# One sum of GpSimd put earlier, the PSUM pools swapped, and a convolution tap given to DVE, in a Hyena layer with experts

## The chip, the cores and the metric

The kernel runs on one core of a Trainium2 chip. Its engines are TensorE (PE, with its weight loads as PEld), VectorE (DVE), ScalarE (ACT), GpSimd (POOL) and SyncE (SP), which here issues most of the transfers. The metric is the device time of one execution in microseconds (us). A profile of one execution stands beside it.

## The reference, cut to what matters

The input is x, 8192 tokens of 512 channels. A first layer projects it to three streams of 512 channels, runs a short convolution of three taps over time on each, multiplies two of them to a gate, convolves the gate with a filter as long as the sequence, and multiplies the outcome by the third stream:

```python
u = x @ W_in + b_in                       # 8192 x 1536
up = pad(u, ((0, 0), (2, 2), (0, 0)))     # over time
uc = up[:, 0:length] * w[:, 0] + up[:, 1:length+1] * w[:, 1] + up[:, 2:length+2] * w[:, 2] + b
x0, x1, v = split(uc, 3)
v = v * x1                                # the gate
k = _gen_filter(...)                      # two sine layers, then the taps with a decay
v = _causal_fft_conv(v, k, filter_bias)
y = (v * x0) @ W_out + b_out
x = layernorm(x + y)
```

A second layer sends each group of 32 tokens to 32 experts in four sets and adds what they give, with a second layer norm. The change does not touch it.

## The kernel before, in words

The kernel has three stages, called one after the other from hyena_then_experts: project (the projection, the short convolution, the filter), convolve (the long convolution as Fourier products on PE) and experts.

**How project is tiled.** Tokens come in 8 blocks of 1024, and the 512 channels of each stream in two pairs (m) of two 128-channel tiles. A Quad is one block, one pair m and one stream s: two tiles of channels by two halves of 512 tokens. There are 8 x 2 x 3 = 48 of them, walked in the loop over j (from L464); r = j % 6 is the place within a block, r = 5 its last quad. A quad is computed in Strassen's way (Winograd's form): seven products in place of eight, each two matmuls of 128x128 by 128x512 (L327). They take sums of weight tiles (sums_of_win) and sums of token tiles:

```python
a, c = {"1": ("12", "11"), "2": ("22", "t1"), "3": ("22", "12"), "4": ("21", "t2")}[name]
x["t" + name] = t = wk.tile(..., bufs=2 if name == "1" else 1)
e.tensor_tensor(t, x[a], x[c], ALU.subtract)      # L206
```

So there are four sums for each block, t1 to t4, each a 128x1024 subtraction; t2, t3 and t4 have one buffer. The token tiles "11", "12", "21", "22" are loaded by SP (load_tokens, L194) into six buffers. The sums for block 0 are made on DVE at the start, those of later blocks on GpSimd: sum 1 in the turn r = 3 of the block before, sums 2, 3 and 4 in its turn r = 5, where also the tile "22" of the next block is loaded, after p1 of that turn.

**The order of a turn.** PE, DVE, ACT and GpSimd follow the order in which the program is written (manual_schedule); SP's order is made by the planner. A turn j issues: p1 (product of "11", copied out by ACT); what is left of the filter's work from the turn before (left); p2 and p6 (into one pair of PSUM banks; p2 reads "21", p6 reads t2; drained by DVE, L346); the short convolution of the quad before (before); p75 (t3, then t1; drained by DVE, L361 and L362); sums 2 and 3 where r = 5; a piece of the filter; p43 (t4 and "22"; drained by DVE, L369); sum 4 where r = 5.

**The short convolution of a quad** (short_convolution): ACT carries two columns over (L377, L378) and writes the tap of the newest token with the bias into four PSUM banks (L389). With on_dve false, ACT also writes the oldest tap into w in SBUF (L395, 128x1024), DVE adds the middle tap (L405) into a tile o in SBUF, and GpSimd adds o to w (L415 for the streams s = 1, 2; L419 for s = 0, where w is kept in two interleaved halves). With on_dve true, DVE adds the middle tap in place in PSUM (L405), and then the oldest tap with a second instruction that reads PSUM and writes w (L409). After that s = 0 is written to memory as x0 (L421), s = 1 is kept, and s = 2 is multiplied with it on GpSimd (L429) and written as the gate (L430). on_dve is true for s = 2 from j = 23 on. The last quad, j = 47, has s = 0; its short convolution stands behind the loop, with on_dve false.

**PSUM.** There are eight banks. In project a pool of four single banks (bank: p1, the filter, the short convolution) is opened first and one of two pairs of banks (pair: p26, p75, p43) second. When both are closed, convolve opens a pool of four pairs over all eight banks (banks, psum2, with reuse_waits="tile").

**The start of convolve.** over_n1 multiplies tiles of the filter's taps by a Fourier table (L552) into those pairs, 16 matmuls of 128x64 by 128x128 a pair (tile pa); DVE (L561) and ACT (L559) copy them in turn into place. That tile fills 192 KB of each partition, over the SBUF that project used.

Every matmul is in fp32 and has two records in the profile, so one product of a quad has four, and one pa tile 32.

Of the kernel before, what the change touches and what calls it, by code (L numbers as in the profile page):

```python
# [15 lines left out]
ALU = mybir.AluOpType  # L16
# [79 lines left out]
@with_exitstack  # L96
def hyena_then_experts(ctx: ExitStack, tc: tile.TileContext, i: dict, out: bass.AP):
    nc = tc.nc

    const = ctx.enter_context(tc.tile_pool(name="const", bufs=1))  # L100
    dram = ctx.enter_context(tc.tile_pool(name="dram", bufs=1, space=bass.MemoryType.DRAM))

    def load(pool, name):
        t = pool.tile(list(i[name].shape), F32, tag=name, name=name + "_sb")
        nc.sync.dma_start(out=t, in_=i[name])
        return t

    def in_dram(what, shape):
        return [dram.tile(shape, F32, tag=f"{what}{ct}", name=f"{what}{ct}") for ct in range(NCT)]


    y_dram = {
        (ct, n): dram.tile([P, BT], F32, tag=f"y{ct}_{n}", name=f"y{ct}_{n}")
        for ct in range(NCT)
        for n in range(NBLK)
    }


    with tc.tile_pool(name="pairs", bufs=2) as pairs, tc.tile_pool(name="in", bufs=3) as tables:
        kept = {  # L120
            name: const.tile(list(i[name].shape), F32, tag=name, name=name + "_sb")
            for name in ("chan", "c_in", "c_back")
        }
        between = in_dram("x0", [P, L]), in_dram("gate", [P, P, N2]), in_dram("taps", [P, P, N2])
        with (
            tc.tile_pool(name="psum1", bufs=4, space=bass.MemoryType.PSUM) as psum,
            tc.tile_pool(name="psum0", bufs=2, space=bass.MemoryType.PSUM) as psum0,
        ):

            def bank(name):  # L130
                return psum.tile([P, 512], F32, tag="ps", name=name)

            def pair(name):
                return psum0.tile([P, 2, TB], F32, tag="pair", name=name)

            project(tc, i, bank, pair, load, between, kept, pairs)
        with tc.tile_pool(
            name="psum2", bufs=4, space=bass.MemoryType.PSUM, reuse_waits="tile"
        ) as psum:

            def banks(name):
                return psum.tile([P, 1024], F32, tag="ps", name=name)

            convolve(tc, i, banks, kept, pairs, tables, between, y_dram)
    experts(tc, i, load, y_dram, out)


def project(tc, i, bank, pair, load, between, kept, small):
# [11 lines left out]
    with (  # L160
# [40 lines left out]
        def sum_of_tokens(b, x, name, e):  # L201
            a, c = {"1": ("12", "11"), "2": ("22", "t1"), "3": ("22", "12"), "4": ("21", "t2")}[name]
            x["t" + name] = t = wk.tile(
                [P, 2, TB], F32, tag=f"xs{name}", name=f"xs{name}_{b}", bufs=2 if name == "1" else 1
            )
            e.tensor_tensor(t, x[a], x[c], ALU.subtract)  # L206
# [166 lines left out]
        def short_convolution(q, on_dve):  # L373

            b, m, s = q.b, q.m, q.s
            now = carry[:, s, :, m]
            nc.scalar.copy(q.u[:, :, 0:2], now)  # L377
            nc.scalar.copy(now, q.u[:, :, 2 * TB : 2 * TB + 2])  # L378
            for half in range(2):
                ct = m + NP * half  # L380
                u = q.u[:, 1 - half]
                at = s * NCT + ct
                w = wk.tile([P, 2 * TB], F32, tag="w", name=f"w_{half}{q.nm}", bufs=5)

                by_half = lambda v: v.rearrange("p (a h b) -> p h a b", h=2, b=N2 // 2)
                pss = [bank(f"o_{half}_{n}{q.nm}") for n in range(2)]
                for n in range(2):
                    t0 = n * TB
                    nc.scalar.activation(  # L389
                        pss[n], u[:, t0 + 2 : t0 + 2 + TB], AF.Identity,  # L390
                        bias=bias[:, at : at + 1], scale=ch[:, at, 4:5],
                    )
                if not on_dve:
                    of = u[:, 0 : 2 * TB]
                    nc.scalar.activation(  # L395
                        w if s else w.rearrange("p (h a b) -> p h a b", h=2, b=N2 // 2),
                        of if s else by_half(of), AF.Identity, scale=ch[:, at, 2:3],
                    )
                for n in range(2):
                    t0, ps = n * TB, pss[n]  # L400
                    if on_dve:
                        o = ps
                    else:
                        o = wk.tile([P, TB], F32, tag="o", name=f"o_{half}_{n}{q.nm}", bufs=4)
                    nc.vector.scalar_tensor_tensor(  # L405
                        o, u[:, t0 + 1 : t0 + 1 + TB], ch[:, at, 3:4], ps, ALU.mult, ALU.add
                    )
                    if on_dve:
                        nc.vector.scalar_tensor_tensor(  # L409
                            w[:, t0 : t0 + TB], u[:, t0 : t0 + TB], ch[:, at, 2:3], o,  # L410
                            ALU.mult, ALU.add,
                        )
                    elif s:
                        wn = w[:, t0 : t0 + TB]
                        nc.gpsimd.tensor_tensor(wn, o, wn, ALU.add)  # L415
                    else:
                        a = TB // N2
                        wn = w.rearrange("p (h a b) -> p h a b", h=2, b=N2 // 2)[:, :, n * a : (n + 1) * a]
                        nc.gpsimd.tensor_tensor(wn, by_half(o), wn, ALU.add)  # L419
                if s == 0:  # L420
                    nc.sync.dma_start(  # L421
                        out=x0_dram[ct].rearrange("c (h n) -> c h n", h=2)[:, :, b * TB : (b + 1) * TB],
                        in_=w.rearrange("c (h n) -> c h n", h=2),
                    )
                elif s == 1:
                    gates[half] = w
                else:
                    gate = gates.pop(half)
                    nc.gpsimd.tensor_tensor(gate, gate, w, ALU.mult)  # L429
                    nc.sync.dma_start(  # L430
                        out=gate_dram[ct][2 * b * TB // N2 : 2 * (b + 1) * TB // N2].rearrange(
                            "a c b -> c a b"
                        ),
                        in_=gate.rearrange("c (a b) -> c a b", b=N2),
                    )
# [28 lines left out]
        for j in range(n_quads):  # L464
            b, r = divmod(j, 3 * NP)
            m, s = r // 3, (1, 2, 0)[r % 3]
            if r == 0 and b:
                x, nxt = nxt, None
            if j < 3:
                q = quads[j]  # L470
            else:
                q = Quad(b, m, s, x)
                q.p1()
                if r == 5 and nxt:
                    load_tokens(b + 1, nxt, ("22",))
            for f in left:
                f()
            if j >= 2:
                q.p2()
                q.p6()  # L480
            if before:
                short_convolution(before, before.s == 2 and j > filter_until)
            if j == 1:
                sums_of_win(1, nc.gpsimd)
            q.p75()
            if r == 5 and nxt:
                sum_of_tokens(b + 1, nxt, "2", nc.gpsimd)
                sum_of_tokens(b + 1, nxt, "3", nc.gpsimd)
            if j < filter_until:
                n = n_filter * (j + 1) // filter_until - n_filter * j // filter_until  # L490
            else:
                n = taps_by_turn[r]
            parts, rides = [f(*args) for f, *args in rides[:n]], rides[n:]
            left = []
            if j >= filter_until and parts:
                parts.pop(0)()()
            q.p43()
            for on_dve in parts:
                left.append(on_dve())
            before = q  # L500
            if b + 1 < NTB // 2:
                if r == 1:
                    nxt = {}
                    load_tokens(b + 1, nxt, ("12", "11", "21"))
                if r == 3:
                    sum_of_tokens(b + 1, nxt, "1", nc.gpsimd)
                if r == 5:
                    sum_of_tokens(b + 1, nxt, "4", nc.gpsimd)
        for f in left:
            f()  # L510
        short_convolution(before, False)


CC = 16
# [661 lines left out]
```

## Time and profile before

| what | before |
|---|---|
| median of 3 runs | 2284.95 us (2281.37 to 2286.8) |
| the profiled execution, its own time | 2284.01 us |
| its span, first to last instruction | 2282.2 us |
| mean granted TensorE clock | 0.965 |
| busy, PE, DVE, ACT, POOL | 2084.2, 1366.3, 800.5, 683.7 us |
| project, from the start to the first matmul of convolve | to 702.05 us |
| convolve, to the first matmul of the experts | to 1417.46 us |

A row of a timeline gives the start in us, the length in us, the engine, the line of the kernel, the operation, the tiles it writes and reads, and how many instructions were merged. What stands in brackets is the idle time of the engine before the row and the instruction that ended it ("<-POOL xs L206": the engine stood until POOL had written xs at L206). A row of the costliest groups ends with busy time, mean ns of one instruction, and the group's idle time with its main releaser. The granted clock is the share of full TensorE clock that the chip let through.

### The profile page before, as it was taken

Reading aid. Unit: us, or ns where it says so; the run is one execution under the profiler, and the core shown is the slowest. Engines: PE = TensorE matmul, PEld = TensorE weight load, DVE = VectorE, ACT = ScalarE, POOL = GpSimd, SP = SyncE. Lnnn points to the kernel's source line nnn. Section 1 sums busy time; section 2 is a strip of 40 time slices with the busy share of each in tenths; the row PEclk is TensorE's granted clock in tenths of the full one; section 3 lists DMA queues with packets and bytes.
Section 4 is the critical chain, followed back from the end, with each engine's and each line's share of the span. In section 5 each row is a group of like instructions: output and inputs, shape, how many; then the busy total and the mean of one; then the engine's idle time right before and its main releaser. Section 6 shows DMA issues by size and latency. Waiting matters only on the chain. (4 is left out here: it accounts for less than half of the span.)

```text
span 2282.2 us, 65661 instructions
## 1 busy us (share of the span) xinstructions
PE 2084.2 (91%) x29472; PEld 1440.4 (63%) x29472; DVE 1366.3 (60%) x1860; ACT 800.5 (35%) x1278; POOL 683.7 (30%) x610
## 2 busy tenths in 40 slices
PE   8898999999998999999999998889988999898765
PEld 3343344444447989999999998355555556555643
DVE  6676776766664643553463463456566666666647
ACT  2444445555553321321331231121343234234333
POOL 3545646766751430340250160211100100110000
PEclk9999999999999999999999999999998999899887
DMA  5312312532434736645655574526663754665373
GB/s 150 102 47 65 94 55 74 193 130 74 139 129 130 223 132 220 211 162 196 194 205 178 177 244 164 157 77 196 217 201 127 246 188 140 196 231 189 114 264 127
DMA packets 188197, 362.61 MB, mean 159 GB/s; under 512 B 78422, under 2 KB 101852, under 8 KB 184844
## 3 DMA queue, kind: packets, MB, share of 16 engines
q1 hardware_dynamic: 182412, 340.05, 46.2%
q10 hardware_dynamic: 5504, 18.35, 2.1%
q8 instruction: 232, 3.80, 0.7%
q14 instruction: 49, 0.40, 0.1%
HBM read 274.47 MB, written 83.89 MB: 157 GB/s over the span
## 5 line engine op out<-in xcount | busy, mean ns | idle before, releaser
L327 PE MATMUL p<-xs,win 128*128 128x512 f32 x768 | 359.6, 613 | 18.6 <-POOL xs L206 16.3
L327 PEld LDWEIGHTS p<-xs,win 128*128 128x128 f32 x768 | 145.9, 194 | 205.2 <-issue 168.8
L327 PE MATMUL p<-xq,win 128*128 128x512 f32 x576 | 259.5, 598 | 7.6 <-DMA win<-in_W_in 5.1
L747 POOL TENSOR_TENSOR xt<-xt,b_outb_sb 128x512 f32<-128x512 f32 x64 | 82.6, 1291 | 608.0 <-DMA xt<-in_x 431.8
L749 PE MATMUL po<-wout,yt 128*128 128x512 f32 x512 | 242.5, 618 | 21.4 <-DVE x L753 18.1
L598 POOL TENSOR_TENSOR place<-t,hs 128x256 f32<-128x256 f32 x132 | 94.7, 718 | 471.9 <-DVE hs L596 470.1
L552 PE MATMUL pa<-c_in_sb,vk 128*64 128x128 f32 x4096 | 226.1, 274 | 9.1 <-DVE o L405 8.7
L552 PEld LDWEIGHTS pa<-c_in_sb,vk 128*64 128x64 f32 x4096 | 224.8, 138 | 10.5 <-DVE o L405 9.5
L576 PE MATMUL px<-place,tab 128*64 128x128 f32 x4096 | 227.8, 273 | 1.9 <-ACT place L559 1.9
L576 PEld LDWEIGHTS px<-place,tab 128*64 128x64 f32 x4096 | 226.2, 136 | 3.0 <-ACT place L559 2.9
L327 PEld LDWEIGHTS p<-xq,win 128*128 128x128 f32 x576 | 110.0, 192 | 149.8 <-issue 135.9
L749 PEld LDWEIGHTS po<-wout,yt 128*128 128x128 f32 x512 | 94.7, 195 | 133.4 <-issue 99.6
L415 POOL TENSOR_TENSOR w<-o,w 128x512 f32<-128x512 f32 x92 | 114.5, 1272 | 173.6 <-ACT w L395 126.4
L561 DVE COPY place<-pa 128x1024 f32<-128x1024 f32 x64 | 78.3, 1224 | 142.2 <-PE pa L552 136.1
L912 ACT COPY si<-pi 128x1024 f32<-128x1024 f32 x96 | 92.9, 1013 | 185.9 <-PE pi L903 128.8
L559 ACT COPY place<-pa 128x1024 f32<-128x1024 f32 x64 | 64.8, 1012 | 252.4 <-PE pa L552 246.6
L405 DVE SCALAR_TENSOR_TENSOR o<-u,chan_sb,o 128x512 f32<-128x512 f32 x192 | 135.8, 744 | 27.2 <-ACT o L389 27.2
L916 DVE STREAM_TRANSPOSE si<-si 128x2048 f32<-128x2048 f32 x48 | 108.1, 2290 | 69.7 <-ACT si L912 69.7
L389 ACT ACTIVATE o<-u,bias,chan_sb 128x512 f32<-128x512 f32 x192 | 141.0, 767 | 0.0
L609 PE MATMUL pz<-c_back_sb,place 64*128 64x128 f32 x2048 | 123.2, 283 | 14.4 <-POOL place L598 14.4
L609 PEld LDWEIGHTS pz<-c_back_sb,place 64*128 64x128 f32 x2048 | 122.5, 199 | 15.4 <-POOL place L598 15.4
L591 ACT COPY hs<-px 128x512 f32<-128x512 f32 x132 | 75.6, 573 | 156.6 <-PE px L576 151.2
(110 smaller groups left out, 3130.1 us busy)
## 6 DMA issues: line engine op xcount, KB each, us to landing
f<-in_f SPq DMA_DIRECT2D x160, 512.0 KB, 5.1
tab<-in_c_mid SPq DMA_DIRECT2D x64, 512.0 KB, 3.8
place<-in_c_out SPq DMA_DIRECT2D x64, 512.0 KB, 4.7
gate<-w SPq DMA_DIRECT2D x32, 512.0 KB, 4.1
x<-w SPq DMA_DIRECT2D x32, 512.0 KB, 3.0
taps<-taps SPq DMA_DIRECT2D x4, 4096.0 KB, 11.1
vk<-taps SPq DMA_DIRECT2D x32, 512.0 KB, 3.6
vk<-gate SPq DMA_DIRECT2D x32, 512.0 KB, 3.7
```

What stands on the lines that cost most here:

```text
L327: nc.tensor.matmul(ps, win[self.m][:, slot, self.s, k, :], self.x[tokens][:, k, :], start=(k == 0), stop=(k == 1),)
L389: nc.scalar.activation(pss[n], u[:, t0 + 2 : t0 + 2 + TB], AF.Identity, bias=bias[:, at : at + 1], scale=ch[:, at, 4:5],)
L405: nc.vector.scalar_tensor_tensor(o, u[:, t0 + 1 : t0 + 1 + TB], ch[:, at, 3:4], ps, ALU.mult, ALU.add)
L415: nc.gpsimd.tensor_tensor(wn, o, wn, ALU.add)
L552: nc.tensor.matmul(ps[r * 64 : (r + 1) * 64, c * N1 : (c + 1) * N1], vk[:, half * 8 + c, :], cin[:, r, :], start=True, stop=True,)
L576: nc.tensor.matmul(ps[h * 64 : (h + 1) * 64, j, :, r, :], tab[:, g % 2 * KC + j, r * 64 : (r + 1) * 64], both[:, :, g * KC + j, h * 64 : ( ...
L598: nc.gpsimd.tensor_tensor(o[:, 0], t[:, 0], hs[:, 1], ALU.subtract)
L609: nc.tensor.matmul(ps[:, h, c, :], spec[rows, r, c0 + c, :], cback[rows, r].rearrange("p q n -> p (q n)"), start=(r == 0), stop=(r == 1),)
L747: nc.gpsimd.tensor_tensor(xt, xt, bout, ALU.add)
L749: nc.tensor.matmul(ps, got["y"][:, ct, t % 2 * P : (t % 2 + 1) * P], wout[:, ct, :], start=(ct == 0), stop=(ct == NCT - 1),)
L912: nc.scalar.copy(o, pss[rr].rearrange("p (r q d) -> p r d q", r=2, q=4))
L916: nc.vector.transpose(turned[:, d].rearrange("p d g -> p (d g)"), stage[:, d].rearrange("p d e -> p (d e)"),)
```

## The change

It has three parts, in project and in hyena_then_experts.

1. In the turn r = 5 of a block, sum 2 of the next block is issued ahead of the short convolution of the quad before, right behind p2 and p6, and no longer behind p75. Sum 3 stays where it was.
2. The pool of pairs is opened ahead of the pool of single banks, so the pairs lie in the first four banks of PSUM and the single banks in the last four.
3. The last short convolution (j = 47, s = 0) is called with on_dve true, and gets a form of the second tap for s = 0 that writes the two interleaved halves of w with two instructions of 256 elements for each 512 tokens.

```diff
         with (
+            tc.tile_pool(name="psum0", bufs=2, space=bass.MemoryType.PSUM) as psum0,
             tc.tile_pool(name="psum1", bufs=4, space=bass.MemoryType.PSUM) as psum,
-            tc.tile_pool(name="psum0", bufs=2, space=bass.MemoryType.PSUM) as psum0,
         ):
...
-                    if on_dve:
+                    if on_dve and s == 0:
+                        a = TB // N2
+                        wv = w.rearrange("p (h a b) -> p h a b", h=2, b=N2 // 2)[:, :, n * a : (n + 1) * a]
+                        for h in range(2):
+                            nc.vector.scalar_tensor_tensor(
+                                wv[:, h], by_half(u[:, t0 : t0 + TB])[:, h], ch[:, at, 2:3],
+                                by_half(o)[:, h], ALU.mult, ALU.add,
+                            )
+                    elif on_dve:
                         nc.vector.scalar_tensor_tensor(
                             w[:, t0 : t0 + TB], u[:, t0 : t0 + TB], ch[:, at, 2:3], o,
                             ALU.mult, ALU.add,
...
             if j >= 2:
                 q.p2()
                 q.p6()
+            if r == 5 and nxt:
+
+                sum_of_tokens(b + 1, nxt, "2", nc.gpsimd)
             if before:
                 short_convolution(before, before.s == 2 and j > filter_until)
             if j == 1:
                 sums_of_win(1, nc.gpsimd)
             q.p75()
             if r == 5 and nxt:
-                sum_of_tokens(b + 1, nxt, "2", nc.gpsimd)
                 sum_of_tokens(b + 1, nxt, "3", nc.gpsimd)
...
         for f in left:
             f()
-        short_convolution(before, False)
+        short_convolution(before, True)
```

## The prediction

> **What bounds the kernel now.** I read the page first: the span is 2282.2 us, TensorE (PE) is busy for 91% of it, no other engine over 60%. So a time is won where PE stands still, and the table of costliest groups says on whom.
>
> ```profile
> PE 2084.2 (91%) x29472; PEld 1440.4 (63%) x29472; DVE 1366.3 (60%) x1860; ACT 800.5 (35%) x1278; POOL 683.7 (30%) x610
> ...
> L327 PE MATMUL p<-xs,win 128*128 128x512 f32 x768 | 359.6, 613 | 18.6 <-POOL xs L206 16.3
> ...
> L552 PE MATMUL pa<-c_in_sb,vk 128*64 128x128 f32 x4096 | 226.1, 274 | 9.1 <-DVE o L405 8.7
> ```
>
> Two idle sums bear on the edits: 16.3 us for token sums made on GpSimd (POOL), 8.7 us at the hand-over from the projection to the convolution. Next, the timeline of PE alone: the 16.3 us are three waits, at the turn from block 0 to 1, 1 to 2 and 2 to 3. The four later block turns have none.
>
> ```profile
> 88.34 5.31 PE L327 MATMUL p<-xq,win 128*128 128x512 f32 x12
> 98.85 8.00 PE L327 MATMUL p<-xs,win 128*128 128x512 f32 x12 [5.20 <-POOL xs L206]
> ...
> 188.56 7.52 PE L327 MATMUL p<-xs,win 128*128 128x512 f32 x12 [6.10 <-POOL xs L206]
> ...
> 275.52 10.12 PE L327 MATMUL p<-xs,win 128*128 128x512 f32 x16 [5.01 <-POOL xs L206]
> ```
>
> The timeline of POOL at the first of them names the sum. PE starts at 98.85, when sum 2 (96.45 + 2.34 = 98.79) is done; ahead of it stand two adds, a gate product, two adds, a gate product, after 10.63 us in which POOL did nothing.
>
> ```profile
> 86.60 2.51 POOL L415 TENSOR_TENSOR w<-o,w 128x512 f32<-128x512 f32 x2 [10.63 <-ACT w L395]
> 89.19 2.36 POOL L429 TENSOR_TENSOR w<-w,w 128x1024 f32<-128x1024 f32 x1
> 91.51 2.48 POOL L415 TENSOR_TENSOR w<-o,w 128x512 f32<-128x512 f32 x2
> 94.07 2.41 POOL L429 TENSOR_TENSOR w<-w,w 128x1024 f32<-128x1024 f32 x1
> 96.45 2.34 POOL L206 TENSOR_TENSOR xs<-xq,xs 128x1024 f32<-128x1024 f32 x1
> 98.75 2.35 POOL L206 TENSOR_TENSOR xs<-xq,xq 128x1024 f32<-128x1024 f32 x1
> ```
>
> A product of the projection is 4 matmul records, about 1.75 us (16 records in 7.03 us at 684.65). Twelve records (p6 and p75) should take 5.2 us; behind the waits they took 8.0 and 7.5. The table by stage shows why: the granted clock is at half after a wait. (Columns: stretch, its length, PE busy and records, granted clock, DMA share, GB/s.)
>
> ```profile
> 93.83:97.25 3.42, 0.00 (x0) 1.00 0.32 70
> 97.25:100.66 3.41, 1.81 (x2) 0.50 0.90 196
> 100.66:104.07 3.41, 3.41 (x5) 0.50 0.72 237
> ...
> 1029.08:1032.50 3.42, 1.70 (x32) 1.00 0.00 0
> ...
> 1175.86:1179.27 3.41, 0.84 (x14) 1.00 1.03 404
> 1179.27:1182.68 3.41, 3.41 (x36) 0.50 0.80 346
> ```
>
> The clock changes at 97.25, 185.99 and 274.74, each 26 x 3.413 us apart, so I cut the stages on that grid. A grid window with 0.84 us of PE work is followed by half clock, one with 1.70 is not.
>
> **Part 1: sum 2 ahead of the short convolution on POOL.** One 2.35 us instruction moves; nothing is added. In its new place it waits for p6 of the last quad of the block (t2 has one buffer) and for the load of the new tokens "22". At block 0 to 1, p6 is done at about 82.0 (its 4 records begin at 80.27). SP issues that load at 78.75, ahead of the gate writes of 91.57, so no queue is passed; the 28 loads of this line land 3.7 to 5.6 us after issue: 82.5 to 84.4. So sum 2 runs from at most 84.4 to 86.7, in the idle time before 86.60. Queued behind it are the two adds, which wait for ACT's w anyway; the delay is 0.1 us at worst. At the next turns the load is issued at 168.08 and 254.96, the adds begin at 176.39 and 263.27: cover of 0.4 us or more. In the four later turns, sum 2 goes between taps and gate products (POOL is idle from 354.08 to 357.79; load issued at 349.72, sum done by 357.7). PE waits for nothing there: worth nothing, costs nothing. Were that cover gone, a delay of the adds would hold back sum 3, the buffers o and w, and so DVE and ACT. DVE beside a busy POOL keeps its pace: three L254 took 2.15 us beside a gate product (94.32) and beside an idle POOL (80.21).
>
> What is late next is sum 3: t3 opens p75. POOL's chain from 86.60 is as it was, so sum 3 falls into sum 2's slot and is done at 98.79, 188.51, 275.47. Sum 4 follows 2.3 us later, before p43 asks for it. PE now does p6 at once:
> - Turn 1: p6 93.65 to 95.4, wait 3.4, p75 98.85 to 102.35; before, p75 ended at 106.85 (DVE L361, which waits for it, starts at 106.88): 4.5 saved.
> - Turn 2: p6 182.45 to 184.2, wait 4.3, p75 to 192.0 against 196.2: 4.2.
> - Turn 3: p6 270.5 to 272.25, wait 3.25, p75 to 279.0 against 283.95: 4.95.
>
> Sum 13.7 us at full clock. DVE can follow: in turn 1 its sine work ends at 97.2, its four L405 by about 102.8, then L361; PE has p43 meanwhile.
>
> Does the clock fall in these shorter waits? The Trainium skill, page "TensorE: Matmul & The Clock Gate", section "HAM oscillation", holds that PE gaps must stay under about 3.4 us. By that rule turns 1 and 3 keep their clock, turn 2 mostly loses it (some 2 us): 12 us saved. The rows speak for less: 0.84 us of work did not hold a window of 3.41. The limit lies between 0.84 and 1.70 us of work; I take the middle, 1.3, so a wait costs the clock once over 2.1 us of it fall in one grid window. The grid's position against the program is not mine to know. A wait of 3.3 escapes only if the edge cuts it nearly in half (about 1 in 4), one of 4.3 hardly ever. The cost of a fall is half the PE time spent at half clock: (1.81 + 3.41)/2 = 2.6 at the first wait of the trace, 2.1 and 3.0 at the others; averaged over the grid's position some 2.0. So 1.5 + 2.1 + 1.4 = 5.0 is lost. **Part 1: 13.7 - 5.0 = 8.7 us**, from 5.6 (all three fall at 2.7) to 13.7 (none).
>
> **Part 2: pairs of banks first in PSUM, and part 3: the last tap on DVE.** They meet at the hand-over.
>
> ```profile
> 695.62 1.23 DVE L369 TENSOR_TENSOR u<-p,u 128x1024 f32<-128x1024 f32 x1
> ...
> 699.85 4.93 POOL L419 TENSOR_TENSOR w<-o,w 128x512 f32<-128x512 f32 x4 [3.69 <-ACT w L395]
> 700.54 1.45 DVE L405 SCALAR_TENSOR_TENSOR o<-u,chan_sb,o 128x512 f32<-128x512 f32 x2 [1.01 <-ACT o L389]
> ...
> 702.05 38.12 PE L552 MATMUL pa<-c_in_sb,vk 128*64 128x128 f32 x670 [8.65 <-DVE o L405]
> ...
> 708.04 2.35 DVE L561 COPY place<-pa 128x1024 f32<-128x1024 f32 x2 [6.05 <-DMA x<-w]
> ```
>
> The first bank pair of the convolution now lies over the single banks of the short convolution, freed by the last L405 (701.99). With the pairs of the projection there instead, PE starts when L369 has read the last one: 696.85. I take it that each new tile waits only for what lay in its place: the expert stage's first po began at 1417.46, while the last py was being read (1417.67 to 1418.95).
>
> But the first copies wait for something else, the x0 write landing at 708.0. Four pa tiles fit in PSUM; the fifth waits for a copy, so for 708.0 + 1.22 = 709.25. Before, the fourth tile ended at 710.6 (its first half at half clock). That caps the gain at 1.35 us.
>
> The last tap: ACT drops two L395 (1.15 each), POOL four adds (4.93), DVE gains eight instructions of 256 elements. No row has that size; it lies between half of L409's 0.75 and 0.75. From L362 (0.69 for 512) against L369 (1.23 for 1024), 256 elements are 0.27 less than 512: 0.48. DVE then needs 4 x (0.75 + 2 x 0.48) = 6.8 us from 698.07, less small overlaps: 704.7 (6.0 to 9.0 us by the two ends, 704.1 to 707.1). POOL ended at 704.78. So x0 lands no sooner. Yet the single banks are held to 704.7 instead of 701.99, since the tap reads them. The third tile may thus wait until then, with a cold clock again: 704.7 plus two tiles (1.75 each at full clock, 3.5 at half) gives 708.2 to 711.7. Gain between +1.35 and -1.1; if the new tiles do wait for everything, PE starts at 704.7 and 3.4 are lost. **I take +0.5.**
>
> **Sum.** 8.7 + 0.5 = 9.2. The profiled execution took 2284.0 us (2282.2 of span and 1.8 around it); that less 9.2 is 2274.8. The median of the three runs is 0.9 above that execution: **2275.7 us**.
>
> **Rivals.**
> - Likeliest (0.50): as above; own range 2271 to 2280.
> - The clock holds in the shorter waits (0.20): 13.7 + 1.3 = 15 saved, 2270. For it: the skill's rule, and waits cut by the grid. Against: the row of 0.84 us.
> - Little left (0.18): all three waits cost their clock in full, the hand-over loses 3.4: 5.6 - 3.4 = 2.2 saved, 2283; with a DVE that follows less well, no change. For it: L405 in turn 1 ends as late as p75.
> - The edit does nothing (0.05): the planner gives PSUM or SP another order and the waits stay: 2285. Against: POOL's order is written by hand.
> - Slower (0.07): POOL stands at the moved sum, waiting for tokens "22", with adds and gate products behind it. Each us of landing after 84.25 delays t3 by one. From 2.9 us (8.7/3) a turn, landing after 87.1, it costs more than it brings; at 5 us it gives 2284.95 + 6.3 = 2291. Against: 8.4 us from issue, where the slowest row has 5.6.
>
> About 0.2% (4.6 us) is what a measurement here can tell from no change. Faster: the first two, and part of the third: 0.78; same 0.15; slower 0.07. Range 2268 to 2283: it reaches below the second case and to the third.
>
> **What would show it.** Right: on POOL, one L206 in the idle time before the adds of each of those turns; on PE, p6 with no wait and a wait of 3 to 4.5 us ahead of p75, for sum 3; at the hand-over, pa records from about 697, a second gap, copies still at about 708 behind x0. Wrong: a POOL wait for xq ahead of L206; waits for sum 3 longer than 4.5 us; full clock behind them (then more is won); pa starting at 704 or later.

## The result and the profile after

The changed kernel takes 2273.72 us (median of 7 runs, 2270.23 to 2280.26), before it was 2282.65 us (7 runs beside them): a ratio of 0.996, 95% interval 0.9943 to 0.9976, and 8.9 us less (9.2 were forecast). The profiled execution took 2273.7 us with a span of 2271.9, 10.3 us less than the one before.

On the changed kernel's page PE stands idle for token sums for 11.2 us (16.3 before), and for 8.0 us at the hand-over from the projection to the convolution (9.1 before, the whole idle time of that row). The added lines have moved L552 to L562, L561 to L571, L415 to L423 and L429 to L437.

```profile
L327 PE MATMUL p<-xs,win 128*128 128x512 f32 x768 | 354.5, 606 | 13.2 <-POOL xs L206 11.2
...
L562 PE MATMUL pa<-c_in_sb,vk 128*64 128x128 f32 x4096 | 227.2, 274 | 8.0 <-DVE w L412 5.4
```

Timeline of PE in the changed kernel, the three block turns. The rows now have 8 records where they had 12 (and 12 where they had 16): p6 has gone ahead of the wait, and what waits is p75.

```profile
99.46 5.12 PE L327 MATMUL p<-xs,win 128*128 128x512 f32 x8 [3.48 <-POOL xs L206]
...
186.32 6.06 PE L327 MATMUL p<-xs,win 128*128 128x512 f32 x8 [4.41 <-POOL xs L206]
...
271.82 7.11 PE L327 MATMUL p<-xs,win 128*128 128x512 f32 x12 [3.30 <-POOL xs L206]
```

Timeline of POOL at the first of them. The first L206 is sum 2, in what was idle time, started by the landing of the tokens "22". The adds follow with a wait of their own for ACT, so sum 2 held nothing back. Sum 3 (97.05) stands where sum 2 stood.

```profile
83.25 2.36 POOL L206 TENSOR_TENSOR xs<-xq,xs 128x1024 f32<-128x1024 f32 x1 [6.68 <-DMA xq<-in_xT]
87.21 2.51 POOL L423 TENSOR_TENSOR w<-o,w 128x512 f32<-128x512 f32 x2 [1.60 <-ACT w L395]
...
97.05 2.35 POOL L206 TENSOR_TENSOR xs<-xq,xq 128x1024 f32<-128x1024 f32 x1
```

The table by stage of the changed kernel, cut on its own grid of 3.413 us (stretch, length, PE busy and records, granted clock, DMA share, GB/s). The clock still fell behind all three waits, twice for one window and once for two.

```profile
95.52:98.94 3.42, 0.46 (x2) 1.00 0.26 57
98.94:102.35 3.41, 2.89 (x4) 0.50 0.98 239
102.35:105.76 3.41, 3.41 (x9) 1.00 0.55 208
180.86:184.28 3.42, 1.05 (x3) 1.00 0.47 102
184.28:187.69 3.41, 1.37 (x2) 0.50 0.77 163
187.69:191.10 3.41, 3.41 (x5) 0.50 0.83 298
269.61:273.02 3.41, 1.20 (x3) 1.00 0.74 156
273.02:276.44 3.42, 3.42 (x5) 0.50 0.92 308
```

The hand-over in the changed kernel (timeline). One pa tile starts 2.3 us behind the last p43, and then PE waits 5.4 us more, for the new second tap (L412).

```profile
680.03 1.88 PE L327 MATMUL p<-xq,win 128*128 128x512 f32 x4
...
684.17 1.97 PE L562 MATMUL pa<-c_in_sb,vk 128*64 128x128 f32 x32 [2.27 <-DVE u L362]
...
691.55 28.71 PE L562 MATMUL pa<-c_in_sb,vk 128*64 128x128 f32 x480 [5.41 <-DVE w L412]
...
696.67 2.35 DVE L571 COPY place<-pa 128x1024 f32<-128x1024 f32 x2 [3.69 <-DMA x<-w]
...
701.08 1.23 DVE L571 COPY place<-pa 128x1024 f32<-128x1024 f32 x1 [2.06 <-PE pa L562]
```

Where the 10.3 us came from, by the times of the same events in the two traces; "new" is what was won since the row above:

| event | before | after | ahead by | new |
|---|---|---|---|---|
| first matmul of the filter at L270 (pf) | 46.0 | 46.6 | -0.6 | -0.6 |
| p75 drained (L361), turn 1 | 106.88 | 104.62 | 2.3 | +2.9 |
| the same, turn 2 | 196.22 | 192.42 | 3.8 | +1.5 |
| the same, turn 3 | 283.96 | 277.25 | 6.7 | +2.9 |
| first long group of taps (L284), ahead of the fourth turn | 357.41 | 347.71 | 9.7 | +3.0 |
| end of the last p43 | 693.40 | 681.91 | 11.5 | +1.8 |
| fifth copy of pa | 712.38 | 701.08 | 11.3 | -0.2 |
| first po | 1417.46 | 1405.8 | 11.7 | +0.4 |
| end | 2282.2 | 2271.9 | 10.3 | -1.4 |

The three turns give 7.3 us. The 3.0 behind turn 3 are the clock: before, it was at half from 339.59 for 6.8 us (behind short waits of the taps' matmuls); in the changed kernel it stayed at full there. The 1.8 behind that come from the four later turns (see the point on them below).

### The profile page after: what moved, and what is told of

It reads as the page before. It is cut to its first block, busy times and chain, and to the rows that moved or that the text cites. A ratio compares the mean times of both kernels' runs of the same rounds, so it can differ in the third digit from the quotient of the medians.

```text
span 2271.9 us, 65665 instructions
## 1 busy us (share of the span) xinstructions
PE 2085.4 (92%) x29472; PEld 1441.6 (63%) x29472; DVE 1372.8 (60%) x1868; ACT 799.0 (35%) x1276; POOL 679.3 (30%) x606
## 5 line engine op out<-in xcount | busy, mean ns | idle before, releaser
L327 PE MATMUL p<-xs,win 128*128 128x512 f32 x768 | 354.5, 606 | 13.2 <-POOL xs L206 11.2
L562 PE MATMUL pa<-c_in_sb,vk 128*64 128x128 f32 x4096 | 227.2, 274 | 8.0 <-DVE w L412 5.4
L562 PEld LDWEIGHTS pa<-c_in_sb,vk 128*64 128x64 f32 x4096 | 225.8, 138 | 9.6 <-issue 9.3
L423 POOL TENSOR_TENSOR w<-o,w 128x512 f32<-128x512 f32 x92 | 114.5, 1273 | 162.8 <-ACT w L395 108.0
L571 DVE COPY place<-pa 128x1024 f32<-128x1024 f32 x64 | 78.3, 1224 | 139.8 <-PE pa L562 136.1
L405 DVE SCALAR_TENSOR_TENSOR o<-u,chan_sb,o 128x512 f32<-128x512 f32 x192 | 136.3, 745 | 29.4 <-ACT o L389 29.4
```

The costliest lines, as they stand in the source:

```text
L327: nc.tensor.matmul(ps, win[self.m][:, slot, self.s, k, :], self.x[tokens][:, k, :], start=(k == 0), stop=(k == 1),)
L405: nc.vector.scalar_tensor_tensor(o, u[:, t0 + 1 : t0 + 1 + TB], ch[:, at, 3:4], ps, ALU.mult, ALU.add)
L562: nc.tensor.matmul(ps[r * 64 : (r + 1) * 64, c * N1 : (c + 1) * N1], vk[:, half * 8 + c, :], cin[:, r, :], start=True, stop=True,)
```

## The experiments

The theory: part 1 carries the gain; sum 3 is what is late next; part of what it leaves is half clock. Rivals: the hand-over carries it, or it was luck of the clock's grid. Times are ratios to runs of the kernel before on the same chip.

**Part 1 alone.** The diff of part 1, nothing else.

> Before plus part 1 alone (sum 2 ahead of the short convolution on GpSimd). Theory (part 1 carries the gain, by less idle time at three block turns and less half clock behind them): the last p43 of project ends near 682, about 11.5 us sooner than before, as in the changed kernel; time 0.9945 to 0.9975 of before. Rival A (the hand-over to the convolution carries it): project ends within 5 us of before, time within 0.2% of before. Rival B (the third part of the gain that lies behind turn 3 was luck of the clock grid): the three waits shrink as in the changed kernel, but project ends only 7 to 9 us sooner.

Measured: 0.9963 (0.9949 to 0.9976), median 2273.44. The waits are 3.49, 4.43 and 3.29 us, the last p43 ends at 682.47. So part 1 alone gives what the whole change gives, and the hand-over is not where it comes from. The half clock at 339.59 was missing here too, so this run does not tell whether those 3.0 us are luck of the grid (rival B).

**Part 2 alone**: the two pool lines exchanged. **Part 3 alone**: the last tap on DVE.

> Before plus part 2 alone (pairs first in PSUM; the last tap stays with ACT and GpSimd). Theory: project is as before (last p43 ends near 693); the first pa tile starts 2.3 us behind that end in place of 8.65, the single banks come free with the last L405 as before, and the stretch from the end of the last p43 to ACT's second copy of pa falls from 17.2 us to about 16, bounded by the landing of x0 plus one copy. Time 0.999 to 1.001 of before. Rival (the clock falls in the second gap): 17 us or more. Rival A (the hand-over carries the gain): 8 us saved.

> Before plus part 3 alone (last tap on DVE, single banks first in PSUM). Theory: the single banks are held until the last L412, some 2.2 us longer, pa starts about 10.5 to 11 us behind the last p43 with a cold clock, and the stretch from there to ACT's second copy of pa grows from 17.2 us to 19 to 20.5; time 1.000 to 1.002 of before. Rival (x0's landing bounds this stretch): it stays at 17.2 or less.

Measured: 1.0001 (0.9988 to 1.0013) and 1.0007 (0.9996 to 1.0018): neither can be told from no change by its time, but the traces show the hand-over. ACT's second copy of pa comes 16.05 us behind the end of the last p43 with part 2 (about 16 were expected) and 20.9 with part 3 (19 to 20.5 expected). Timeline with part 2 alone:

```profile
690.72 1.88 PE L327 MATMUL p<-xq,win 128*128 128x512 f32 x4
...
694.87 1.97 PE L552 MATMUL pa<-c_in_sb,vk 128*64 128x128 f32 x32 [2.27 <-DVE u L362]
...
700.56 7.06 PE L552 MATMUL pa<-c_in_sb,vk 128*64 128x128 f32 x96 [3.72 <-DVE o L405]
...
711.08 1.23 DVE L561 COPY place<-pa 128x1024 f32<-128x1024 f32 x1 [0.94 <-PE pa L552]
```

And with part 3 alone, where pa starts 11.2 us behind the last p43 (690.39), at half clock for 13.65 us from 692.95:

```profile
688.51 1.88 PE L327 MATMUL p<-xq,win 128*128 128x512 f32 x4
...
701.61 33.64 PE L560 MATMUL pa<-c_in_sb,vk 128*64 128x128 f32 x568 [11.22 <-DVE w L412]
...
713.02 1.23 DVE L569 COPY place<-pa 128x1024 f32<-128x1024 f32 x1 [2.27 <-PE pa L560]
```

With part 2 alone the second tile waits for L405, with part 3 alone the first one for L412, which are the readers of the single banks. From the end of the last p43 to the fifth copy of pa it is 19.0 us before, 18.5 with part 2, 22.6 with part 3, 19.2 with both, and 20.4 with part 1 alone (clock at half for 10.24 us there, 6.83 before). By these waits the two parts act against each other: the swap frees one tile early, the tap holds the single banks longer. The 0.5 us of part 2 are within what the clock alone moves here (1.4 us between two kernels with the same hand-over).

**Filling the wait.** In the first turn of blocks 1 to 3, ahead of the real p75:

```diff
                 ps = pair("p75" + self.nm)
+                if self.s == 1 and self.m == 0 and self.b in (1, 2, 3):
+                    self.product(ps[:, 0], A11, "11")
+                    self.product(ps[:, 1], A11, "11")
+                    if self.b == 2:
+                        nc.tensor.matmul(ps[:, 0], win[self.m][:, A11, self.s, 0, :],
+                                         self.x["11"][:, 0, :], start=True, stop=True)
                 self.product(ps[:, 0], S3, "t3")
```

> The changed kernel plus dummy products on PE in the first turn of blocks 1 to 3, ahead of p75, in the wait for t3 (two products of 1.75 us, in block 2 two and a half; their values are overwritten by p75). Theory (half clock behind the waits costs 6 us): no half clock within 8 us of these three turns, p75's eight records take 3.5 us in place of 5.1, 6.1 and some 5.3, and the last p43 ends 5 to 6.5 us sooner than in the changed kernel; time 0.9925 to 0.9955 of before. Rival (the clock costs little, the idle time is all): p75 no faster, time as the changed kernel or slower.

Measured: 1.0024 (1.0014 to 1.0034), 0.2% slower than before, so the forecast of the time failed. Yet where it was to act it did: no half clock behind the three turns, p75 of turn 1 in 3.70 us (timeline of this kernel) where it took 5.12. The last p43 came at 679.24, 2.7 us ahead of the changed kernel and not 5 to 6.5; a fall of the clock at 327.25, which the changed kernel does not have, stands against it.

```profile
100.32 3.70 PE L327 MATMUL p<-xs,win 128*128 128x512 f32 x8
```

The loss lies far behind: from the start of the first po to that of the last pw (first and last products of the expert stage) it takes 847.3 us, where the changed kernel takes 827.4, with the same order of instructions on the other engines. The run answers its question on the clock in the trace, not in the time, and it opens another one.

**Thirteen small matmuls at the start.** As many matmuls as the fill had, of 8 columns, once; then 64 of them.

```diff
+                if self.b == 0 and self.m == 0 and self.s == 1:
+                    for _ in range(13):        # 64 in the second run
+                        nc.tensor.matmul(ps[:, 0, 0:8], win[self.m][:, A11, self.s, 0, :],
+                                         self.x["11"][:, 0, 0:8], start=True, stop=True)
                 self.product(ps[:, 0], S3, "t3")
```

> The changed kernel plus as many matmuls on PE as the filled kernel had (13), but of 8 columns and put once, ahead of the first p75, in front of all block turns; their values are overwritten. If the filled kernel lost its 13 us in the expert stage because the later part of PE's program lies elsewhere in its stream, this one loses there too: 8 to 16 us slower than the changed kernel, with more idle time of PE put down to issue in the expert stage. Rival (the filled kernel lost them by what it did in time): within 3 us of the changed kernel.

> The changed kernel plus 64 matmuls of 8 columns ahead of the first p75 (values overwritten), in place of the 13 of the padded run: 256 instructions of PE where that run had 52. The 13 made the stretch from the first po to the last pw 844 us long, against 827 in the changed kernel. If the loss comes from where the later program lies against a grid of 64 or 256 instructions, that stretch is 824 to 831 us here; if any added matmuls cost it, 840 or more. The 64 themselves take some 15 us ahead of the first block turn.

Measured: 1.0067 (1.0054 to 1.008) with 13, 1.0074 (1.0048 to 1.0099) with 64. The 13 delay the first pf (L264, at 33.0 in the changed kernel) by 6.8 us, and the stretch of the experts is 844.0 us; together nearly all of the 24 us by which this run is slower than the changed kernel (8 to 16 were expected). The 64 delay the first pf by 27.7 us (some 15 had been expected), and that stretch is 828.6. One row of the groups in the expert stage for the changed kernel, for 13, and for 64, in that order: the idle time that no event explains (issue) is 3.2, 16.0 and 3.6 us.

```profile
L913 PE MATMUL pi<-f,h 32*32 32x128 f32 x6144 | 102.4, 287 | 20.2 <-ACT si L922 7.9 <-DVE x L943 7.2 <-issue 3.2
```

```profile
L919 PE MATMUL pi<-f,h 32*32 32x128 f32 x6144 | 104.3, 290 | 28.1 <-issue 16.0 <-DVE x L949 7.2 <-ACT si L928 4.1
```

```profile
L919 PE MATMUL pi<-f,h 32*32 32x128 f32 x6144 | 102.7, 290 | 20.8 <-ACT si L928 8.7 <-DVE x L949 7.2 <-issue 3.6
```

An fp32 matmul leaves four records (two loads, two matmuls), so 64 of them are 256 instructions of PE, and 13 are 52. Added instructions as such do not cost the 17 to 20 us; where the later program then lies in PE's stream does.

The traces also show what PE waits for there. The page lists a DMA queue of kind "instruction". In the changed kernel it moved 232 packets, all of 16,384 bytes, for 59,362 records of PE, which is one for 256; with 64 matmuls more, 256 instructions, it moved one packet more (pages of the changed kernel and of 64):

```profile
q8 instruction: 232, 3.80, 0.7%
```

```profile
q8 instruction: 233, 3.82, 0.7%
```

And two waits of PE put down to issue can stand exactly 256 instructions apart, here 128 matmuls with their 128 loads (timeline of PE with 13):

```profile
2194.11 1.99 PE L882 MATMUL ph<-dT,f 128*32 128x64 f32 x128 [1.85 <-issue]
2199.33 0.68 PE L882 MATMUL ph<-dT,f 128*32 128x64 f32 x30 [3.22 <-issue]
```

Counting PE's instructions from the start of each trace, the waits of over 1 us that stand at this one place of a block of 256 (number 193, counted from 0) are 9 in the changed kernel's stretch (17.3 us in sum), 16 with 13 (36.0), 19 with the fill (40.7) and 10 with 64 (16.8). In these four traces each of them ends 1.1 to 1.6 us after a packet of that queue has landed. All other waits over 1 us come to 46.9, 48.1, 47.2 and 50.3 us, nearly the same. So what the 13 and the fill lost is waiting for instructions. Why the waits are longer where the ends of blocks fall elsewhere in the stage is not traced.

**t1 first.** The two products of p75 exchanged in the changed kernel; the number of instructions stays.

```diff
-                self.product(ps[:, 0], S3, "t3")
                 self.product(ps[:, 1], S1, "t1")
+                self.product(ps[:, 0], S3, "t3")
```

> The changed kernel with the two products of p75 exchanged: t1 first, then t3 (no instruction more or less). Theory (t3 is what is late next, and half clock follows a wait of more than about 2 us): the three waits fall by one product of 1.75 us, from 3.5, 4.4 and 3.3 to 1.7, 2.7 and 1.6; half clock behind the first and third is gone, behind the second it may stay. The last p43 ends 8 to 11 us sooner than in the changed kernel, time 0.991 to 0.9945 of before. Rival (the clock falls behind any wait): only the 5.2 us of idle time are won, 0.9935 to 0.996.

Measured: 0.9919 (0.9904 to 0.9933), median 2263.74. Timeline of PE, and the table by stage:

```profile
99.71 1.98 PE L327 MATMUL p<-xs,win 128*128 128x512 f32 x4 [1.77 <-POOL xs L206]
...
183.46 3.68 PE L327 MATMUL p<-xs,win 128*128 128x512 f32 x4 [2.71 <-POOL xs L206]
...
266.59 1.98 PE L327 MATMUL p<-xs,win 128*128 128x512 f32 x4 [1.58 <-POOL xs L206]
```

```profile
96.58:99.99 3.41, 1.64 (x5) 1.00 0.49 107
99.99:103.40 3.41, 3.41 (x8) 1.00 0.98 282
180.18:183.60 3.42, 0.70 (x3) 1.00 0.45 99
183.60:187.01 3.41, 3.41 (x4) 0.50 0.98 309
```

The waits fall by the length of one product, 5.1 us in all. The clock holds with 1.64 us of work in the window and falls with 0.70. Half clock behind the three turns is now 3.41 us long in sum, 13.65 in the changed kernel. The last p43 ends at 673.86, 8.1 us ahead of the changed kernel. This is the mechanism shown at work: t3 was late next, and half clock came with it.

**Sum 3 ahead as well**, in the changed kernel (its diff is shown); then two kernels built on the one before, with no tap on DVE: **sum 2 ahead, t1 first and pairs first**, and **all of it**, the same with sum 3 ahead as well.

```diff
-                [P, 2, TB], F32, tag=f"xs{name}", ..., bufs=2 if name == "1" else 1
+                [P, 2, TB], F32, tag=f"xs{name}", ..., bufs=2 if name in "13" else 1
-                w = wk.tile([P, 2 * TB], F32, tag="w", ..., bufs=5)
+                w = wk.tile([P, 2 * TB], F32, tag="w", ..., bufs=4)
...
                 sum_of_tokens(b + 1, nxt, "2", nc.gpsimd)
+                sum_of_tokens(b + 1, nxt, "3", nc.gpsimd)
...
             q.p75()
-            if r == 5 and nxt:
-                sum_of_tokens(b + 1, nxt, "3", nc.gpsimd)
```

> The changed kernel with sum 3 ahead of the short convolution too, right behind sum 2; t3 gets a second buffer for it, and w four buffers in place of five to make room. Theory: PE has no wait for token sums at any block turn and no half clock there; the adds start 0.8 to 1.5 us later, which nothing on PE waits for; the last p43 ends 14 to 18 us sooner than in the changed kernel, time 0.988 to 0.991 of before. Rival (GpSimd then is late with sum 4, or w with four buffers holds ACT and DVE back): waits for t4 or for the short convolution take the place, under 8 us won.

> Before plus sum 2 ahead, pairs first in PSUM and t1 first, without the last tap on DVE. Theory: as the run with t1 first, and the hand-over some 0.7 us shorter than in the changed kernel (18.5 in place of 19.2 us from the end of the last p43 to the fifth copy of pa): time 0.9905 to 0.994 of before. Rival (the tap on DVE is needed for the gain at the hand-over): slower than the run with t1 first by over 2 us.

> Before plus sums 2 and 3 ahead (t3 with two buffers, w with four), t1 first in p75, pairs first in PSUM, the last tap left with ACT and GpSimd. Theory: no wait of PE for a token sum over 0.3 us at the block turns and no half clock behind them; the last p43 ends 1 to 3 us sooner than in the better of the runs with t1 first or with sum 3 ahead, the fifth copy of pa 18 to 19 us behind it; time 0.987 to 0.991 of before. Rival (w with four buffers holds the adds back): slower than the run with t1 first and pairs first alone.

Measured: 0.9891 (0.9873 to 0.9909), 0.9916 (0.9902 to 0.993) and 0.9884 (0.9865 to 0.9903), median 2257.86 for the last: 1.2% under the kernel before, and the lowest ratio here, though its interval overlaps that of sum 3 ahead alone. The times are as forecast, the steps only in part. With sum 3 ahead the last p43 ended 9.9 us sooner, not 14 to 18: no wait for t3 is left, but in turn 1 another took the place, that of the filter's matmul for a bank that L405 had to read first (timeline of that kernel), and the clock fell at 102.56 behind it.

```profile
101.29 1.12 PE L264 MATMUL pf<-pe,W1p_sb 6*128 6x512 f32 x2 [1.63 <-DVE o L405]
```

The hand-over took 19.6 us in the last two runs, not 18.5: a wait of 2.1 us for a copy, and half clock again. So the forecast that it gains 0.7 us without the tap did not come true.

## Why the prediction was right, point by point

- **Sum 2 fits into GpSimd's idle time: right.** It ended at 85.6, the adds began at 87.21 on ACT's account. The slower case needed 8.4 us from issue to landing; the loads of tokens landed 6.1 us after issue at most.
- **Sum 3 is late next: right.** Waits of 3.4, 4.3 and 3.25 us were forecast, 3.48, 4.41 and 3.30 measured; the run with t1 first shows it by its effect.
- **The clock falls in these waits: right, against the rule.** The rule of some 3.4 us (the Trainium skill, page "TensorE: Matmul & The Clock Gate", section "HAM oscillation") would have kept it in turn 3 (3.30), and it fell. It fell behind all three; the chance that a wait of 3.3 us escapes, put at 1 in 4, did not come about. Forecast at 5.0 us, this cost half of 2.89, of 1.37 + 3.41 and of 3.42: 5.5.
- **The limit of 0.84 to 1.70 us of work in a window: too simple.** Both of its rows are of matmuls of 64 rows (L609). Where PE did only products of the projection, the clock fell with up to 1.22 us of work (part 1 alone, window from 270.17) and held from 1.51 on (part 2 alone, from 92.89), so 1.3 served for these waits. But in the trace before, windows with 2.02 and 1.75 us of work fell as well (from 145.03 and 336.18, ahead of the half clock at 339.59); they have matmuls of 6 and of 64 rows in them. Busy time alone does not decide; what does is not shown.
- **Part 1, 8.7 us: 7.3 measured at the three turns.** The term was 1.4 too large: 0.5 of it is the clock and 0.2 the waits, which were a little longer; the rest is not traced.
- **"PE waits for nothing there: worth nothing" for the four later turns: wrong.** PE stood there too, in gaps that the view of waits lists for PE's weight loads (PEld) and not for its matmuls. p6 and p75 of the fourth turn, timelines of before and of the changed kernel:

```profile
365.46 5.68 PE L327 MATMUL p<-xs,win 128*128 128x512 f32 x12
...
367.44 0.30 PEld L327 LDWEIGHTS p<-xs,win 128*128 128x128 f32 x2 [0.93 <-POOL xs L206]
```

```profile
355.77 5.31 PE L327 MATMUL p<-xs,win 128*128 128x512 f32 x12
```

  Twelve records took 0.4 us more where sum 3 ended at 367.39, inside them. The periods of three turns alternate by it (from one group of taps to the next such: 399.58 to 441.30 is 41.72, 441.30 to 483.48, with a block turn in it, is 42.18); after the change they are all 41.7. Four times 0.45 is the 1.8 us of the table. So a term that the prediction put at nothing was worth 1.8 us. The sign of it stood in the trace before: the weight loads waited 19 times for these sums, the matmuls 4 times; after the change both wait 4 times.
- **Hand-over, +0.5: -0.2 measured.** That x0's landing caps the gain held: the first copy comes 14.6 us behind the last p43 in both traces. That new tiles wait only for what lay in their place held too. That the first two lie over the pairs did not: the second pa tile waited for L412, which reads a single bank. The size of L412 was right: two of them took 0.87 us, against 0.96.
- **What was not in the sum**: 3.0 us from a fall of the clock (at 339.59) that the changed kernel's trace does not have, and 1.4 lost again in the experts. In the runs with the waits as before, that fall came once (part 2 alone, at 338.65) and once not (part 3 alone); of the nine profiles with part 1 in them, the changed kernel's included, two have one near that place (the fill at 327.25, 64 matmuls at 359.32). Whether the change itself moves it is open. The forecast of 2275.7 is near the measured 2273.7 partly by luck: a term too large, one missing and the fall of the clock offset each other.

## What to carry to other kernels

When an engine in written order makes several inputs for a waiting one, moving the first of them ahead shifts the wait to the second; look also at the consumer's order, which here gave as much again (0.996 to 0.992) by exchanging two lines. Price a wait of TensorE with the half clock behind it, by the work in the window and not by the length of the gap alone; at the block turns here, waits of 2.71 us and more cost it and those of 1.77 and less did not, but other short waits did where small matmuls stood beside them. Check an experiment that adds instructions to TensorE against one that adds as many elsewhere, since the time may come from where the program lies.

## What the runs showed of the hardware that was not expected

Thirteen small matmuls (52 PE instructions) put at the start of the program made the expert stage, over a millisecond later, 17 us longer (844.0 against 827.4), 13 full ones spread over three turns 20 us (847.3), and 64 small ones (256 instructions) 1.2 us (828.6). The Trainium skill, page "Runtime: NRT & Kernel Launch", section "Instruction fetch mechanics", says that instructions are refilled in blocks of 256 and that the crossing is mostly hidden. The period fits: packets of 16,384 bytes, one for 256 instructions, and the waits at one place of each block. The cost is not hidden here: in this stage such waits of over 1 us come to 17.3 us in the changed kernel and 40.7 in the worst; in the kernels without added matmuls they range from 10.1 to 22.5. A difference of some us between two kernels can thus come from where the program lies.
